# Attention's output products placed in the bank of the softmax sums, in halves between later score units; six buffers of probabilities in place of eight

## The chip, the cores and the metric

The kernel runs on one core of a Trainium2 chip (trn2). The metric is the device time of one execution in microseconds (us). One more execution was taken with the hardware profiler; all lines of profiles below come from such an execution. PE is TensorE (matmuls), DVE is VectorE, ACT is ScalarE, POOL is GpSimd, SP is the engine whose queue issues most DMAs.

## The reference, cut to what matters

The program is two transformer layers over 2048 tokens of width 512 in float32. Layer 0 is linear attention beside a mixture of experts, layer 1 is causal attention within a window beside a second block that works on selected tokens. The change lies in the last part of layer 1, its attention with 16 heads of 32:

```python
mask = (q_idx >= k_idx) & (q_idx - k_idx <= WINDOW)          # WINDOW = 1024
scores = jnp.einsum('bhqd,bhkd->bhqk', q, k) / np.sqrt(HD)
scores = jnp.where(mask[None, None, :, :], scores, NEG)
attn = jax.nn.softmax(scores, axis=-1)
out = jnp.einsum('bhqk,bhkd->bhqd', attn, v)
out = out.transpose(0, 2, 1, 3).reshape(b, n, H)
return jnp.einsum('bnh,hm->bnm', out, w_out)
```

The result of that last product is added to everything else that layer 1 computes (kept in a DRAM tensor `res_d`) and written out.

## The kernel before, in words

Queries, keys and the row maxima of the scores are ready (transposed, on chip) when the last stage begins. It works on **groups** `(Q, g)`: Q is a block of four query tiles (512 queries), g a set of four heads. The order of groups is (2,0), (0,0), (2,1), (0,1), (2,2), (0,2), (2,3), (0,3), then (1,0) to (1,3), then (3,0) to (3,3). A group is a list of **units**, each one block of 128 keys against up to 512 queries: nine units for Q=2 and Q=3, four for Q=0, eight for Q=1.

For each unit the loop does this:

- `probabilities` (L1300 scores on PE, L1315 the negated maxima added by a matmul, L1323 the masks added by a matmul) fills two score tiles `ps`, each two PSUM banks; `ps_s` has three such buffers. ACT takes the exponential into SBUF (L1334): into `acc` for the first unit of a group, into `pt` for the others. `pt` has eight buffers, two a unit.
- `values` (L1374) multiplies the previous unit's probabilities with V into `av`, one PSUM bank that a group keeps. After the last unit ACT copies it into `aT` (L117).
- `gathered` (L1407) adds the previous unit's probabilities into `acc`, on POOL for odd units and on DVE for even ones, both halves one after the other. For Q=2 and Q=3 the last unit goes straight into the sums on PE.
- `ending` of the previous group is a generator, advanced once a unit: three empty steps, then the sums over keys by a matmul with ones (L1388) into `sm`, a single PSUM bank, then for each query tile a reciprocal (L1417) and a multiplication of `aT` (L1418), two tiles a step. If the group was the last of its query block (g=3), the four `output`s follow, one a step.
- `output` (L1337 to L1349) loads a tile of `res_d` (two buffers `res`), multiplies `aT` with `w_out` in four matmuls (L1344) into `po`, which is one of the three score buffers, adds `res` on DVE (L1348) and stores.

The units are software pipelined: in the turn of unit n PE runs the scores of n, then the values of n-1, then what `ending` holds. When the last unit of a group is through, whatever is left of the group before's ending is run to its end. Groups of Q=0 have four units, so the ending of (2,3) is still at its reciprocals when (0,3) is over, and all four outputs of Q=2 are then issued together. The outputs of Q=0 come in the units of (1,0), those of Q=1 in the units of (3,0), those of Q=3 after the last unit.

[...] A layer that records the program settles the order of each engine's instructions when the kernel is built; it may place an instruction some places away from where the source has it. A buffer of a pool is handed on when the last instruction that used it has ended, by a semaphore wait of the new user.

Of the kernel before, what the change touches and what calls it, by code (L numbers as in the profile page):

```python
# [12 lines left out]
F32 = mybir.dt.float32  # L13
# [6 lines left out]
P = 128  # L20
T = 2048
NT = T // P
D = 512
NC = D // P
# [14 lines left out]
def two_layer_kernel(ctx: ExitStack, tc: tile.TileContext, a: dict, out: bass.AP):  # L39
# [29 lines left out]
    def load(eng, dst, src):  # L69
        eng.dma_start(out=dst, in_=src)  # L70
# [57 lines left out]
    with ExitStack() as l0:  # L128
# [208 lines left out]
        with ExitStack() as p3:  # L337
            wk = p3.enter_context(tc.tile_pool(name="wk3", bufs=2, reuse_waits="tile"))
# [5 lines left out]
            def mm(name):  # L344
                return ps.tile([P, TB], F32, tag="mm", name=name)
# [119 lines left out]
            for b in range(NTB):  # L465
# [39 lines left out]
                if b == NTB - 1:  # L505
# [3 lines left out]
                    def pool(name, bufs):  # L509
                        return p4.enter_context(  # L510
                            tc.tile_pool(name=name, bufs=bufs, side="right", reuse_waits="tile")
                        )
# [33 lines left out]
                for i in range(TB // P):  # L546
# [4 lines left out]
                    po = mm(f"po_{b}_{i}")  # L551
# [171 lines left out]
    with p4:  # L723
        wka, r5, wk = pool("wka", 2), pool("r5", 1), pool("wk4", 2)
# [272 lines left out]
    with ExitStack() as p5:  # L997
        f5 = p5.enter_context(tc.tile_pool(name="f5", bufs=1, side="right", reuse_waits="tile"))
        fw = p5.enter_context(tc.tile_pool(name="fw", bufs=5, side="right", reuse_waits="tile"))
        wk = p5.enter_context(tc.tile_pool(name="wk6", bufs=2, side="right", reuse_waits="tile"))  # L1000
# [223 lines left out]
        for ch in range(NFC):  # L1224
            wd = stream(a["w_down"][ch * D : (ch + 1) * D, :], f"wd_{ch}")
            for i in range(NC):
                f = ch * NC + i
# [34 lines left out]
        )  # L1262
    w_out = const([P, NC, D], "w_out", vo_pool)
    load(nc.sync, w_out, a["w_out"].rearrange("(c p) o -> p c o", p=P))
    pt = ctx.enter_context(tc.tile_pool(name="pt", bufs=8, reuse_waits="tile"))
    acc_pool = ctx.enter_context(tc.tile_pool(name="acc_pool", bufs=2, reuse_waits="tile"))
    wk = ctx.enter_context(tc.tile_pool(name="wk7", bufs=2, reuse_waits="tile"))
    ps_s = ctx.enter_context(tc.tile_pool(name="ps_s", bufs=3, **tight))
    ps_v = ctx.enter_context(tc.tile_pool(name="ps_v7", bufs=1, **tight))

    QT = 4
# [63 lines left out]
            got.append(pT)  # L1335
        return got

    def output(i, aT, j0):
        rows = slice(i * P, (i + 1) * P)
        res = wk.tile([P, D], F32, tag="res", name=f"res_{i}")  # L1340
        load(nc.sync, res, res_d[rows, :])
        po = ps_s.tile([P, D], F32, tag="s", name=f"po_{i}")
        for g in range(NC):
            PE.matmul(  # L1344
                po, aT[:, g, j0 : j0 + P], w_out[:, g, :], start=g == 0, stop=g == NC - 1
            )
        o = wk.tile([P, D], F32, tag="o", name=f"o_{i}")
        V.tensor_tensor(o, po, res, ALU.add)  # L1348
        load(nc.sync, out[rows, :], o)  # L1349

    class Group:

# [55 lines left out]

        def ending(self):

            Q, g, aT = self.Q, self.g, self.aT
            for _ in range(3):
                yield
            self.sums(self.acc, 0, QT * P, True)
            for j in range(QT):
                js = slice(j * P, (j + 1) * P)
                V.reciprocal(self.sm[:, js], self.sm[:, js])  # L1417
                V.tensor_tensor(aT[:, g, js], aT[:, g, js], self.sm[:, js], ALU.mult)  # L1418
                if j % 2:
                    yield  # L1420
            if g == NC - 1:
                for j in range(QT):
                    output(QT * Q + j, aT, j * P)
                    yield

    pending, ending = None, iter(())

# [2 lines left out]
    outputs = {}  # L1430
    for Q, g in order:
        if g == 0:
            outputs[Q] = wk.tile([P, NC, QT * P], F32, tag="aT", name=f"aT_{Q}")
        group = Group(Q, g, outputs[Q])
        for n, unit in enumerate(group.us):
            name = f"{Q}_{g}_{n}"
            got = probabilities(g, unit, name, n == 0)
            if (Q, g, n) == (2, 0, 1):

                early.place(ps_s, "s", 0.0)  # L1440
                early.turned()
            if pending is not None:
                pending[0].values(*pending[1:])
                pending[0].gathered(*pending[1:])
                if pending[1] == len(pending[0].us) - 1:
                    for _ in ending:
                        pass
                    ending = pending[0].ending()
            next(ending, None)
            pending = (group, n, got)  # L1450
# [3 lines left out]
        pass  # L1454
    for _ in group.ending():
        pass


def _rope(n, dim):
# [48 lines left out]
```

## Time and profile before

| what | value |
|---|---|
| median of 3 runs | 1708.75 us (1707.05 to 1709.91) |
| the profiled execution | 1708.32 us, span 1706.6 us |
| mean granted clock of TensorE | 0.995 |
| instructions | 20413 |
| last stage, from the first score matmul at 1328.0 us | about 378 us |
| its scores, L1300 | 1152 records, 139.9 us busy |
| its values from `pt`, L1374 | 1024 records, 100.8 us busy |
| its exponentials, L1334 | 208 into `pt`, 181.6 us busy |
| its accumulations, L1407 | POOL 110, 252.8 us; DVE 80, 144.4 us |

How to read a profile: the page gives busy times of each engine, then the chain of work that ended last, then the costliest groups of instructions, each by line of the kernel, engine, operation, tiles and shape. A timeline line gives the start and the duration in us, then engine, line, operation, tiles, shapes and how many instructions were merged (float32 matmuls are recorded as two), and in brackets the time that the engine was idle before it and what ended that. A row by stage gives the length of a stretch, the busy time of PE, of PE's weight loads, of DVE, ACT and POOL (with counts), then the granted clock of TensorE as a share of full speed, then DMA.

### The profile page before, as it was taken

Reading aid. Unit: us, or ns where it says so; the run is one execution under the profiler, and the core shown is the slowest. Engines: PE = TensorE matmul, PEld = TensorE weight load, DVE = VectorE, ACT = ScalarE, POOL = GpSimd, SP = SyncE. Lnnn points to the kernel's source line nnn. Section 1 sums busy time; section 2 is a strip of 40 time slices with the busy share of each in tenths; the row PEclk is TensorE's granted clock in tenths of the full one; section 3 lists DMA queues with packets and bytes.
Section 4 is the critical chain, followed back from the end, with each engine's and each line's share of the span. In section 5 each row is a group of like instructions: output and inputs, shape, how many; then the busy total and the mean of one; then the engine's idle time right before and its main releaser. Section 6 shows DMA issues by size and latency. Waiting matters only on the chain.

```text
span 1706.6 us, 20413 instructions
## 1 busy us (share of the span) xinstructions
PE 1656.3 (97%) x8114; PEld 742.5 (44%) x8114; DVE 982.1 (58%) x1256; ACT 589.3 (35%) x939; POOL 499.5 (29%) x398
## 2 busy tenths in 40 slices
PE   8999999999999999989999989999999999999999
PEld 3445444444444444444443434454564333433343
DVE  4754746344444544356676676775554477556565
ACT  3213333243253344212121110440100576447473
POOL 3230000000000200043565425230000677558584
PEclk9999999999999999999999999999899999999999
DMA  9411001120030421121010024112222300110101
GB/s 361 170 38 47 25 25 37 45 92 25 25 111 25 94 104 50 50 69 50 32 26 32 28 99 173 62 50 74 75 99 75 99 1 2 50 51 2 50 1 38
DMA packets 62384, 109.23 MB, mean 64 GB/s; under 512 B 12528, under 2 KB 14064, under 8 KB 61520
## 3 DMA queue, kind: packets, MB, share of 16 engines
q1 hardware_dynamic: 55856, 106.12, 18.2%
q0 software_dynamic: 1152, 1.21, 0.4%
q10 hardware_dynamic: 5280, 0.59, 0.4%
q8 instruction: 63, 1.03, 0.2%
q14 instruction: 33, 0.27, 0.1%
HBM read 86.24 MB, written 21.67 MB: 63 GB/s over the span
## 4 chain that ended last, share of the span: by engine, by line
PE 80%; DVE 11%; ACT 2%; DMA 2%; POOL 2%; issue 2%; SPq 0%; DVEq 0%; POOLq 0%; ACTq 0%
PE acc L478 6%; PE eg L492 6%; PE ea L494 6%; PE ps L1300 6%; PE pa L633 6%; PE av L1374 6%; PE p L965 5%; PE po L553 3%; PE pq L367 3%; PE po L1344 3%; PE gx L242 3%; DVE mx L645 3%; PE mg L1214 2%; PE pao L1176 2%; PE pm L1229 2%
## 5 line engine op out<-in xcount | busy, mean ns | idle before, releaser
L645 DVE TENSOR_REDUCE mx<-pa 128x4 f32<-128x1536 f32 (+3 forms) x144 | 252.8, 1756 | 151.7 <-PE pa L641 71.9
L1407 POOL TENSOR_TENSOR acc<-acc,pt 128x1024 f32<-128x1024 f32 (+2 forms) x110 | 252.8, 2327 | 96.6 <-DVE acc L1407 43.3
L1334 ACT ACTIVATE pt<-ps 128x1024 f32<-128x1024 f32 (+3 forms) x208 | 181.6, 925 | 107.9 <-PE ps L1323 61.4
L1407 DVE TENSOR_TENSOR acc<-acc,pt 128x1024 f32<-128x1024 f32 (+1 forms) x80 | 144.4, 1833 | 103.9 <-POOL acc L1407 103.9
L633 PE MATMUL pa<-kT,qT 32*128 32x384 f32 (+3 forms) x1152 | 139.4, 539 | 19.5 <-DVE mx L645 15.8
L350 ACT ACTIVATE r_e<-eg 128x512 f32<-128x512 f32 x128 | 76.0, 595 | 201.6 <-PE eg L492 194.8
L1300 PE MATMUL ps<-qT,kT 32*128 32x512 f32 (+3 forms) x1152 | 139.9, 524 | 0.0
L352 DVE TENSOR_TENSOR h<-ea,r_e 128x512 f32<-128x512 f32 x128 | 87.3, 684 | 85.2 <-ACT r_e L351 84.6
L743 POOL TENSOR_TENSOR cosg<-cosg,gam 128x512 f32<-128x512 f32 x2 | 2.5, 1269 | 442.7 <-DVE gam L740 442.7
L492 PE MATMUL eg<-xl,rwgT 128*128 128x512 f32 x256 | 130.7, 592 | 0.0
L494 PE MATMUL ea<-xw,rw1T 128*128 128x512 f32 x256 | 130.7, 592 | 0.0
L478 PE MATMUL acc<-h,rw2T 128*128 128x512 f32 x256 | 129.3, 592 | 0.0
L965 PE MATMUL p<-w_qk,xnt 128*128 128x512 f32 x256 | 123.7, 606 | 2.3 <-DVE qk L758 2.2
L1374 PE MATMUL av<-pt,v 128*32 128x512 f32 (+3 forms) x1024 | 100.8, 482 | 0.0
L1300 PEld LDWEIGHTS ps<-qT,kT 32*128 32x128 f32 x1152 | 54.7, 183 | 94.7 <-issue 65.8
L633 PEld LDWEIGHTS pa<-kT,qT 32*128 32x128 f32 x1152 | 46.7, 184 | 103.7 <-DVE mx L645 66.8
L488 DVE TENSOR_TENSOR xw<-xw,xl 128x512 f32<-128x512 f32 x64 | 43.8, 685 | 82.8 <-DMA xw<-w_d 82.7
L351 ACT ACTIVATE r_e<-r_e 128x512 f32<-128x512 f32 x128 | 80.5, 631 | 5.7 <-ACT r_e L350 1.9
L494 PEld LDWEIGHTS ea<-xw,rw1T 128*128 128x128 f32 x256 | 48.6, 190 | 61.2 <-issue 59.3
L492 PEld LDWEIGHTS eg<-xl,rwgT 128*128 128x128 f32 x256 | 48.6, 190 | 61.2 <-issue 60.7
L478 PEld LDWEIGHTS acc<-h,rw2T 128*128 128x128 f32 x256 | 48.6, 190 | 61.2 <-issue 54.7
L763 POOL TENSOR_TENSOR t<-qk,cosg 128x1024 f32<-128x1024 f32 x15 | 35.3, 2353 | 99.6 <-DVE qk L758 63.4
(336 smaller groups left out, 2444.2 us busy)
## 6 DMA issues: line engine op xcount, KB each, us to landing
xw<-w_d SPq DMA_DIRECT2D x64, 256.0 KB, 3.2
x<-in_x SPq DMA_DIRECT2D x16, 256.0 KB, 4.3
res_d<-x SPq DMA_DIRECT2D x16, 256.0 KB, 2.6
xr<-res_d SPq DMA_DIRECT2D x16, 256.0 KB, 4.1
xn_d<-xn SPq DMA_DIRECT2D x16, 256.0 KB, 3.0
res_d<-xr SPq DMA_DIRECT2D x16, 256.0 KB, 3.1
xnq<-xn_d SPq DMA_DIRECT2D x16, 256.0 KB, 2.7
v_d<-vt SPq DMA_DIRECT2D x16, 256.0 KB, 2.0
```

What stands on the lines that cost most here:

```text
L351: S.activation(r, r, AF.Square)
L352: V.tensor_tensor(dst, pa, r, ALU.mult)
L478: PE.matmul(acc, rw2T[:, j, e, :], h, start=e == 0 and j == 0, stop=e == E - 1 and j == 1,)
L492: PE.matmul(pg, rwgT[:, e, hb], xl, start=True, stop=True)
L494: PE.matmul(pa, rw1T[:, e, hb], xw, start=True, stop=True)
L633: PE.matmul(pS[:, h, : w * P], qT[r, g, i * P : (i + 1) * P], kT[r, g, ks], start=True, stop=not (edge or last),)
L645: V.tensor_reduce(mx[:, g, :, c], pS[:, :, : w * P], AX.X, ALU.max)
L965: PE.matmul(pj, xnt[:, c, :], w, start=c == 0, stop=c == NC - 1)
L1300: PE.matmul(pS[h // 2][:, h % 2, t0 * P - q0 : (t1 + 1) * P - q0], kT[r, g, kb * P : (kb + 1) * P], qT[r, g, t0 * P : (t1 + 1) * P], start ...
L1334: S.activation(pT[:, :, :n], pS[hp][:, :, :n], AF.Exp)
L1374: PE.matmul(self.av[h * HD : (h + 1) * HD, t0 * P - o : (t1 + 1) * P - o], vs[kb // 4][:, kb % 4, hs], got[h // 2][:, h % 2, t0 * P - q0 : ...
L1407: eng.tensor_tensor(part, part, got[hp][:, :, : q1 - q0], ALU.add)
```

## The change

- `output` becomes a generator of two halves: a load of `res`, the allocation of `po` and two of the four matmuls, then (one step later) the other two, the addition and the store. Its PSUM tile is given by the caller.
- When a group of g=3 ends, its four outputs are put on a list `ready`. Each later `ending` takes up to two of them after its own reciprocals, into the bank of the sums (`ps_v`, tag `sm`). So the outputs of Q=2 and Q=0 run in the endings that pass through (1,0), (1,1), (1,2) and (1,3) (on into the group that follows), those of Q=1 in (3,1) and (3,2). What is left at the end, the four of Q=3, runs in score buffers as before.
- When a group is through, the rest of the ending before it is run ahead of `gathered`, not behind it, since for Q=2 and Q=3 `gathered` of a last unit takes the bank of the sums.
- `pt` has six buffers in place of eight; `aT` has three in place of two, since an attention output now lives on into later groups. The two sizes cancel in SBUF.

```diff
-    pt = ctx.enter_context(tc.tile_pool(name="pt", bufs=8, reuse_waits="tile"))
+    pt = ctx.enter_context(tc.tile_pool(name="pt", bufs=6, reuse_waits="tile"))
...
-    def output(i, aT, j0):
+    def output(i, aT, j0, pool, tag):
+
         rows = slice(i * P, (i + 1) * P)
         res = wk.tile([P, D], F32, tag="res", name=f"res_{i}")
         load(nc.sync, res, res_d[rows, :])
-        po = ps_s.tile([P, D], F32, tag="s", name=f"po_{i}")
+        po = pool.tile([P, D], F32, tag=tag, name=f"po_{i}")
         for g in range(NC):
             PE.matmul(
                 po, aT[:, g, j0 : j0 + P], w_out[:, g, :], start=g == 0, stop=g == NC - 1
             )
+            if g == 1:
+                yield
         o = wk.tile([P, D], F32, tag="o", name=f"o_{i}")
         V.tensor_tensor(o, po, res, ALU.add)
         load(nc.sync, out[rows, :], o)
+        yield
+
+    ready = []
...
+            for _ in range(min(2, len(ready))):
+                yield from output(*ready.pop(0), ps_v, "sm")
             if g == NC - 1:
-                for j in range(QT):
-                    output(QT * Q + j, aT, j * P)
-                    yield
+                ready.extend((QT * Q + j, aT, j * P) for j in range(QT))
...
-            outputs[Q] = wk.tile([P, NC, QT * P], F32, tag="aT", name=f"aT_{Q}")
+            outputs[Q] = wk.tile([P, NC, QT * P], F32, tag="aT", name=f"aT_{Q}", bufs=3)
...
                 pending[0].values(*pending[1:])
-                pending[0].gathered(*pending[1:])
-                if pending[1] == len(pending[0].us) - 1:
+                last = pending[1] == len(pending[0].us) - 1
+                if last:
                     for _ in ending:
                         pass
+                pending[0].gathered(*pending[1:])
+                if last:
                     ending = pending[0].ending()
...
+    for args in ready:
+        for _ in output(*args, ps_s, "s"):
+            pass
```

## The prediction

> **What bounds the kernel now.** I read the page first (busy shares, then the chain that ended last), then the busy time by stage, the waits of PE, and last the order of time around one output projection.
>
> ```profile
> PE 1656.3 (97%) x8114; PEld 742.5 (44%) x8114; DVE 982.1 (58%) x1256; ACT 589.3 (35%) x939; POOL 499.5 (29%) x398
> ...
> PE 80%; DVE 11%; ACT 2%; DMA 2%; POOL 2%; issue 2%; SPq 0%; DVEq 0%; POOLq 0%; ACTq 0%
> ```
>
> PE is the engine to watch. The change touches only the last stage, from about 1328 us. Its row by stage, and the waits of PE in it:
>
> ```profile
> core 0: us, PE busy (x) PEld busy (x) DVE busy (x) ACT busy (x) POOL busy (x), PEclk, DMA share, GB/s
> 1328.00:1706.00 378.00, 372.69 (x3405) 142.45 (x3404) 232.30 (x227) 220.29 (x257) 255.44 (x112) 1.00 0.10 33
> ```
>
> ```profile
> engine line waited for: us in total, times, longest us
> PE po L1344 <- DVE o L1348: 1.5, 2, 1.3
> ```
>
> PE is busy for 372.69 of 378 us. Of the 5.3 us idle, about 4 are the drain after the last matmul and 1.5 are two waits of an output projection for the addition of an earlier one. So the end is the sum of what PE executes, in its own order; a microsecond that PE stands still is a microsecond on the time, and the most that a better order can return is small.
>
> Now one group with outputs, Q=1, g=0 (units n=0 to 7). First PE, then DVE, same microseconds:
>
> ```profile
> 1483.79 1.06 PE L1374 MATMUL av<-acc,v 128*32 128x512 f32 x8
> 1484.79 1.36 PE L1300 MATMUL ps<-qT,kT 32*128 32x512 f32 x8
> ...
> 1489.51 1.04 PE L1388 MATMUL sm<-acc,ones_f 128*32 128x512 f32 x8
> ...
> 1494.35 1.06 PE L1374 MATMUL av<-pt,v 128*32 128x512 f32 x8
> 1495.34 3.70 PE L1344 MATMUL po<-w_out,aT 128*128 128x512 f32 x8
> 1498.97 0.71 PE L1300 MATMUL ps<-qT,kT 32*128 32x256 f32 x8
> ```
>
> ```profile
> 1487.45 4.51 DVE L1407 TENSOR_TENSOR acc<-acc,pt 128x1024 f32<-128x1024 f32 x2 [4.14 <-POOL acc L1407]
> 1491.88 0.95 DVE L1417 RECIPROCAL sm<-sm 128x128 f32<-128x128 f32 x1
> ...
> 1495.83 0.97 DVE L1417 RECIPROCAL sm<-sm 128x128 f32<-128x128 f32 x1
> 1496.71 1.21 DVE L1407 TENSOR_TENSOR acc<-acc,pt 128x1024 f32<-128x1024 f32 x1
> 1497.83 0.27 DVE L1418 TENSOR_TENSOR aT<-aT,sm 128x128 f32<-128x128 f32 x1
> ```
>
> PE has written the sums by 1490.5, but DVE is still inside unit 2's accumulation until 1491.95, then walks through four reciprocals and multiplications, with a piece of unit 4's accumulation ahead of the fourth multiplication. It leaves the bank of the sums at 1498.10. PE came to the output at 1495.34 and started, because its target is one of the three score buffers.
>
> **The change, part by part.**
>
> *Work.* The same 16 outputs: 64 matmuls, 3.63 us of PE each output (1495.34 to 1498.97), 16 additions of 0.69 us, 16 loads and 16 stores. Nothing is added or removed; the last four outputs stay at the end with their tail. In SP's queue the loads still stand two ahead, and the next load behind a store is needed a group later, so no load becomes late.
>
> *Where they go.* Two outputs in each of the groups (1,0), (1,1), (1,2), (1,3), (3,1), (3,2), in halves of 1.82 us ahead of units 6, 7, 8 and of the unit after (for Q=1, which has eight units, the last two are the next group's units 0 and 1). I checked this on the built order of instructions.
>
> *The added wait.* The first half now needs the bank of the sums, so it waits for DVE's fourth multiplication (in the built program that is the instruction it waits for). From the end of the values product of unit 0 I count both paths. PE to the output's place: 1484.79 to 1495.34 = 10.55 us (10.51 in (1,1), 10.77 in (3,1), read in the same way). DVE: unit 1's accumulation on POOL starts at 1485.05, unit 2's on DVE ends 6.90 us later at 1491.95, the fourth multiplication 6.15 us after that: 1498.10, so 13.3 us (13.3 in (1,1) and in (3,1)). With about 0.1 us from DVE to PE (sums at the end start 0.12 us after the accumulation they wait for), PE stands still 13.4 - 10.55 = 2.85 us in each of four Q=1 groups and 13.4 - 10.77 = 2.65 us in two Q=3 groups: 11.4 + 5.3 = **16.7 us**. Behind the waiting matmul on PE are unit 6's scores, for which ACT, POOL and DVE wait in turn; nothing else feeds PE. The bounds: zero if DVE were done in time; 4 to 5 us each if accumulation lags as it does in (1,2) and (1,3) of before, where the fourth multiplication came 14.4 and 15.6 us after unit 0's values. I take 2.85, because the stall and the 7.3 us of outputs let POOL and DVE catch up before the next group.
>
> *The second wait.* The second output waits for the first one's addition, which in DVE's order stands behind both accumulations of unit 6. For Q=1 these end 5.75 us after the fourth multiplication (1550.66 to 1556.41 in (1,2)); with the addition 6.4 us. PE, after the stall, comes back after 1.82 + 1.87 + 1.82 + 1.39 = 6.9 us (the two stretches between are 1565.57 to 1567.44 and on to 1568.83). For Q=3 the same rows of (3,2) and (3,1) give 8.6 against 1.82 + 2.96 + 1.82 + 2.84 = 9.4 us. Covered in both, by 0.5 to 0.8 us: I take 0, bound 0.5 each (3 us in all). The sums of a Q=3 group's last unit wait for the second addition, done 0.8 us after its product, while PE has 2.5 us of other work ahead: 0.
>
> *What goes away.* The two waits in (3,0), 1.47 us. Also a hidden one: at a boundary between groups, unit 1's stretch on PE takes 3.11 us (1551.96 to 1555.07) against 2.28 where an output stood before it (1515.10 to 1517.38), because PE waits inside its matmuls for ACT's exponentials and copy. A half output now covers it at three boundaries, (1,1) to (3,0): -2.5 us. At (0,3) to (1,0), where the burst of four outputs (14.0 us at 1468.58) covered it, it appears: +0.83. Together **-3.1 us**. The burst itself had PE busy throughout, so dissolving it returns nothing.
>
> *Six buffers.* An exponential now waits for the accumulations of three units before, not four. Laying the exponentials' starts beside the accumulations' ends, in the Q=2 groups only the first has late ones: unit 8's second half starts at 1353.14, its buffer would be free at 1354.39; two more are late by 0.2 and 0.4 us. In the late Q=1 groups up to 2 us are late in before, but there the outputs now push the exponentials back by over 4 us. I take **+0.5 us**, bounds 0 and 2.
>
> *The clock.* A still PE can lose its clock. Windows of 3.4 us of before, and what followed:
>
> ```profile
> 765.36:768.76 3.40, 1.49 (x17) 1.02 (x18) 2.32 (x5) 0.19 (x1) 3.32 (x3) 1.00 0.00 0
> 768.77:772.17 3.40, 3.40 (x17) 1.58 (x16) 0.80 (x1) 1.57 (x3) 0.45 (x1) 0.50 0.04 11
> ...
> 908.72:912.12 3.40, 1.60 (x7) 0.50 (x9) 3.26 (x4) 0.47 (x1) 0.00 (x0) 1.00 0.01 2
> 912.13:915.53 3.40, 3.40 (x18) 1.59 (x11) 2.71 (x3) 0.59 (x1) 3.22 (x2) 1.00 0.02 5
> ```
>
> A gap of 2.69 us (before 767.27) left PE 1.49 us of work in a window of 3.4, and for the next 3.4 us the granted clock was 0.50. Of six such windows with 1.47 to 1.61 us of work, three were followed by 0.50 (the other two begin at 1000.88 and 1195.44). The Trainium skill ("TensorE: Matmul & The Clock Gate", Part 1: The HAM clock gate) halves the clock only after an idle window of about 3.4 us; by it a stall of 2.8 us is safe and this item is 0. The trace shows gaps of 1.8 to 2.7 us punished, so I follow the trace. A stall of 2.8 us placed at random against windows of 3.4 us leaves less than about 1.6 us of work in one of them in two cases of three: an estimate of 4 halved stretches from 6 stalls, each costing half of the 3.0 us or so that lie after the stall, 1.5 us: **+6.0 us**; bounds 0 and 6 x 1.7 = 10.
>
> *Sum.* 16.7 - 3.1 + 0.5 + 6.0 = 20.1 us. The profiled execution took 1708.32 us (span 1706.6), 0.4 us under the median of 1708.75, so against the median: 1708.75 + 20.1 = 1728.9, **1729 us**.
>
> **The rivals.**
>
> - *Stalls at full clock.* The skill's rule holds here, at most one stretch is halved: 20.1 - 6.0 = 14.1, so 1722.9 us. For it: three windows of 1.5 to 1.6 us of work went unpunished.
> - *No stall, not slower.* DVE leaves the bank in time, and only the removed waits count: -3.1 + 0.5 = -2.6, 1706.1 us. This needs DVE's 13.3 us after unit 0's values to shrink under 10.5, by more than two of the 1.3 us reciprocal steps; from there each group is free. For it: the accumulations of 2.3 us hold 1.2 us of work when POOL is quiet (1496.71). Against: POOL's accumulation of unit 3 runs beside them as before, and four groups of before show the 6.15 us after unit 2 unchanged.
> - *Six buffers bind.* If each of four Q=2 groups loses the first one's worst 1.25 us, that is +5 in place of 0.5, with the stalls as above: 1733.4 us. Against: the later three groups show 0.3 us or more of slack.
>
> **How the numbers follow.** A run of three can tell about 0.2%, 3.4 us, from no change. Chances: forecast 0.66, stalls at full clock 0.17, six buffers binding too 0.08, no stall 0.09. The last ends at -0.15%, within 0.2% or just beyond with less cost of buffers: same 0.05, faster 0.04. Slower is 0.91. The range: below, the full-clock case with stalls of 2 us instead of 2.8 gives 1718; above, six halved stretches and 0.5 us at every second wait give 1729 + 4 + 3 = 1736. I state 1718 to 1736, which leaves out the case without stalls and some tails.
>
> **What would show it.** In the profile of the changed kernel: waits of the output matmul for DVE's sums multiplication, six of 2.6 to 2.9 us, 16 to 17 in all; the waits for the output's addition near 0; granted clock 0.50 for 3.4 us after some of these; the stretch of unit 1 at 2.28 us in (1,2), (1,3) and (3,0); ACT waiting for POOL under 2 us. The forecast is wrong if those waits are absent or under 1 us (DVE's chain shortens), if the clock stays at 1.00 after all six, or if PE waits for ACT in the Q=2 groups.

## The result, and the profile after

The changed kernel takes 1733.63 us (median of 4 runs, 1730.32 to 1738.48). The kernel before, run beside it, takes 1709.33 us (4 runs, 1707.05 to 1710.17). The ratio is 1.0148, with a 95% interval of 1.0134 to 1.0162: some 24 us slower. The forecast was 1729 us. The profiled executions are those of 1708.32 us (span 1706.6) and 1730.32 us (span 1728.6).

First the page of the changed kernel: busy shares of the engines, then the chain that ended last.

```profile
PE 1661.9 (96%) x8114; PEld 741.2 (43%) x8114; DVE 972.9 (56%) x1256; ACT 588.4 (34%) x939; POOL 497.8 (29%) x398
...
PE 79%; DVE 11%; DMA 2%; issue 2%; POOL 2%; ACT 2%; SPq 0%; DVEq 0%; ACTq 0%; POOLq 0%
```

PE executes the same 8114 instructions and is still the engine that sets the end, but it is now busy for 5.6 us more, and it stands still. The last stage alone, by busy time, and the waits of PE in it:

```profile
core 0: us, PE busy (x) PEld busy (x) DVE busy (x) ACT busy (x) POOL busy (x), PEclk, DMA share, GB/s
1325.52:1728.60 403.08, 382.53 (x3405) 142.83 (x3404) 222.94 (x227) 220.23 (x257) 253.61 (x112) 0.98 0.10 31
```

```profile
engine line waited for: us in total, times, longest us
PE po L1345 <- DVE aT L1425: 16.3, 6, 2.8
```

From its first score matmul to the end of the span the stage takes 403.1 us in place of 378.6, so **24.5 us** more. Six waits make 16.3 us of that; the two waits of before, for an addition, are gone. PE's busy time in the stage grew by 9.8 us, although its work is the same and its granted clock is down from 1.00 to 0.98.

One group with outputs, (1,1), in order of time. First PE, then DVE in the same microseconds.

```profile
1506.43 1.07 PE L1380 MATMUL av<-pt,v 128*32 128x512 f32 x8
...
1509.00 1.07 PE L1380 MATMUL av<-pt,v 128*32 128x512 f32 x8
1512.86 3.06 PE L1345 MATMUL po<-w_out,aT 128*128 128x512 f32 x4 [2.80 <-DVE aT L1425]
1515.85 1.23 PE L1300 MATMUL ps<-qT,kT 32*128 32x256 f32 x8
...
1518.28 1.98 PE L1345 MATMUL po<-w_out,aT 128*128 128x512 f32 x4
1520.19 0.50 PE L1300 MATMUL ps<-qT,kT 32*128 32x128 f32 x8
```

```profile
1502.16 4.50 DVE L1413 TENSOR_TENSOR acc<-acc,pt 128x1024 f32<-128x1024 f32 x2 [4.15 <-POOL acc L1413]
1506.59 0.95 DVE L1424 RECIPROCAL sm<-sm 128x128 f32<-128x128 f32 x1
...
1511.41 1.21 DVE L1413 TENSOR_TENSOR acc<-acc,pt 128x1024 f32<-128x1024 f32 x1
1512.54 0.27 DVE L1425 TENSOR_TENSOR aT<-aT,sm 128x128 f32<-128x128 f32 x1
...
1518.25 1.29 DVE L1413 TENSOR_TENSOR acc<-acc,pt 128x512 f32<-128x512 f32 x2 [4.31 <-ACT pt L1334]
1520.30 0.69 DVE L1351 TENSOR_TENSOR o<-po,res 128x512 f32<-128x512 f32 x1 [0.75 <-PE po L1345]
```

The fourth multiplication of the sums ends at 1512.81 and the output starts at 1512.86. PE was there 2.80 us earlier. Once the stall is paid, everything after it is in time: DVE is done with unit 6's accumulation before the first output's second half ends, and the addition at 1520.30 follows that half at once. Note also the two half outputs: the first lasts from 1512.86 to 1515.85, 2.99 us, the second from 1518.28 to 1520.19, 1.91 us. Most of the first ran at half clock. Rows by stretch of the trace of after: a stall and what follows it, another stall and what follows it, and what follows a third:

```profile
1479.50:1482.90 3.40, 0.59 (x5) 0.22 (x2) 3.33 (x6) 0.81 (x2) 1.84 (x2) 1.00 0.00 0
1482.92:1486.30 3.38, 3.38 (x8) 0.85 (x7) 0.84 (x1) 0.00 (x0) 3.38 (x2) 0.50 0.02 5
...
1571.66:1575.07 3.41, 1.98 (x8) 0.75 (x8) 2.51 (x4) 0.00 (x0) 2.09 (x1) 1.00 0.00 0
1575.07:1578.48 3.41, 3.41 (x28) 1.41 (x28) 1.64 (x2) 1.09 (x2) 2.54 (x2) 1.00 0.00 0
...
1626.28:1633.00 6.72, 5.91 (x24) 2.29 (x24) 1.89 (x3) 0.00 (x0) 5.69 (x2) 0.50 0.00 0
```

Four of the six stalls are followed by a granted clock of 0.50: for 3.41 us from 1482.91, 1513.63 and 1544.35, and for 6.83 us from 1626.27. After the stalls at 1570.57 and 1662.76 (2.52 us each) the clock stays at 1.00. PE is busy for about 16.2 of these 17.1 us, and half of that, 8.1 us, is lost. The last section comes back to why four and not six.

### The profile page after: what moved, and what is told of

Read it like the earlier page. It is cut to its first block, busy times and chain, and to the rows that moved or that the text cites. A ratio compares the mean times of both kernels' runs of the same rounds, so it can differ in the third digit from the quotient of the medians.

```text
span 1728.6 us, 20425 instructions
## 1 busy us (share of the span) xinstructions
PE 1661.9 (96%) x8114; PEld 741.2 (43%) x8114; DVE 972.9 (56%) x1256; ACT 588.4 (34%) x939; POOL 497.8 (29%) x398
## 4 chain that ended last, share of the span: by engine, by line
PE 79%; DVE 11%; DMA 2%; issue 2%; POOL 2%; ACT 2%; SPq 0%; DVEq 0%; ACTq 0%; POOLq 0%
PE eg L492 6%; PE ea L494 6%; PE acc L478 6%; PE ps L1300 6%; PE pa L633 6%; PE av L1380 5%; PE p L965 5%; PE po L1345 4%; PE po L553 3%; PE pq L367 3%; PE gx L242 3%; DVE mx L645 3%; PE mg L1214 2%; PE pm L1229 2%; PE po L555 2%
## 5 line engine op out<-in xcount | busy, mean ns | idle before, releaser
L1413 DVE TENSOR_TENSOR acc<-acc,pt 128x1024 f32<-128x1024 f32 (+1 forms) x80 | 134.8, 1713 | 119.3 <-POOL acc L1413 85.9
L1345 PE MATMUL po<-w_out,aT 128*128 128x512 f32 x128 | 66.6, 655 | 16.3 <-DVE aT L1425 16.3
```

Source lines behind the costliest of these rows:

```text
L1345: PE.matmul(po, aT[:, g, j0 : j0 + P], w_out[:, g, :], start=g == 0, stop=g == NC - 1)
L1413: eng.tensor_tensor(part, part, got[hp][:, :, : q1 - q0], ALU.add)
```

## The experiments

Eleven kernels were run. They ask in turn: are the stalls and the clock what the time is made of; what makes the bank late; is it the bank alone; and is there something in the change that is worth keeping. Each ratio is against the kernel before, run beside it. "The stage" is always the time from the first score matmul of the last stage to the end of the span, in the profiled execution: 378.6 us before, 403.1 us after.

### Six buffers alone (e2_before6)

The kernel before, with one size changed:

```diff
-    pt = ctx.enter_context(tc.tile_pool(name="pt", bufs=8, reuse_waits="tile"))
+    pt = ctx.enter_context(tc.tile_pool(name="pt", bufs=6, reuse_waits="tile"))
```

> The kernel before with six probability buffers and nothing else. My theory (the slow-down is the wait of the outputs for the bank of the sums, and the clock that is lost after it): between 0 and +2 us against before (late exponentials in the first Q=2 group and in the Q=1 groups, part of it hidden), ACT's wait for POOL in the last stage rises from 1.1 to 3 to 8 us, PE's only wait stays that for the addition (1.5 us). Rival (six buffers are what costs): +10 us or more.

Measured: 1710.71 us, ratio 1.0007 (0.9999 to 1.0014). ACT waits for POOL's accumulations 2.7 us in all and PE shows no wait. The stage takes 379.7 us, 1.1 us more, of which the groups (1,2) and (1,3) take 1.0 and 1.2 us more and (3,0) 1.7 us less. The four groups of Q=2 together take 0.3 us more. Six buffers are not where 24 us went.

### The stalls filled with work (e3_fill)

The changed kernel, with three matmuls of no use into a score buffer ahead of the first output of each of the six groups, so that PE is kept busy while the bank of the sums is held:

```diff
+            if ready:
+                fill = ps_s.tile([P, 2, QT * P], F32, tag="s", name=f"fill_{Q}_{g}")
+                for c in range(3):
+                    PE.matmul(
+                        fill[:, 0, :], w_out[:, c, 0:P], w_out[:, c, :], start=c == 0, stop=c == 2
+                    )
             for _ in range(min(2, len(ready))):
                 yield from output(*ready.pop(0), ps_v, "sm")
```

> The changed kernel with three extra matmuls (2.7 us, into a score buffer that nobody reads) just ahead of the first output of each of the six groups, so that PE works while it would stand still. The result is not changed. Theory that part of the loss is the granted clock: the six waits shrink to about 0.1 us each, no stretch of 0.50 follows them, mean clock back to 0.995, and the time falls by 6 to 9 us from the changed kernel's 1733.6 to about 1726, and its runs lie closer together. Rival (the clock costs nothing, all is the wait itself): the time stays within 2 us of 1733. Second rival (PE's order is not the bound): the added 16 us of matmuls make it slower.

Measured: 1727.31 us, ratio 1.0106 (1.0092 to 1.0121). PE in the group (1,1) of this kernel:

```profile
1510.53 2.84 PE L1431 MATMUL fill<-w_out 128*128 128x512 f32 x6
1513.38 1.98 PE L1345 MATMUL po<-w_out,aT 128*128 128x512 f32 x4
1515.30 0.71 PE L1300 MATMUL ps<-qT,kT 32*128 32x256 f32 x8
```

The fill takes the place of the stall (2.84 us against 2.80), and the output starts the moment it ends. No stretch of the stage is at half clock. The stage takes 395.2 us: 7.9 us less than in the changed kernel, though the order of the real work and the time until the bank comes free are the same. That is about what the half clock costs. The stage is still 16.6 us longer than before: the six fills, which only keep PE busy until the bank is free, make 17.0 us, and the small terms summed up under "Why the prediction was right" (-3.1, +0.2, +2.3) make the rest, to within 0.2 us.

### The outputs one unit later (e4_late1)

```diff
+            if ready:
+                yield
             for _ in range(min(2, len(ready))):
                 yield from output(*ready.pop(0), ps_v, "sm")
```

> The changed kernel with one more empty step ahead of the outputs of a group, so that PE comes to the bank of the sums one unit later. Theory: the wait in the Q=1 groups falls from 2.8 to 0.9 us each (unit 6's stretch of 1.87 us lies before it), in the Q=3 groups to 0, and the sums of a Q=3 group's last unit now wait some 0.9 us for the second addition, twice; all waits of PE 5 to 6 us, no halved clock, time about 1712. Rival (spreading the outputs is itself what costs, or the six buffers): stays above 1725.

Measured: 1716.09 us, ratio 1.0033 (1.0020 to 1.0045); no half clock in the stage. Waits of PE in it:

```profile
PE po L1345 <- DVE aT L1425: 3.4, 4, 0.9
```

A unit of scores and values (1.87 us for Q=1, more for Q=3) goes into the stall: 2.5 to 2.8 us become 0.6 to 0.9 in the four groups of Q=1, and the two of Q=3 have none. The stage takes 384.2 us, 5.6 us more than before. The waits explain 3.4 of it; in (3,1) and in (3,2) two score matmuls ahead of the last unit's sums last 1.05 us where they take some 0.3 (the sums follow the second output's addition by 0.25 us), which the list of waits does not show: about 1.5 us for both. In the groups of Q=1 the second output now stays whole (3.70 us at 1495.00, for one), since the group is over before its halves get separate turns. So eight outputs are in halves and cost 1.5 us (the price of halves is given under "Why the prediction was right"). With +0.2 and -3.1 from there too, that makes 3.5 us; 2.1 us I could not assign.

### The bank alone, at the old places (e5_bank)

The kernel before, with all its outputs in the bank of the sums, whole and where they were (the last four, at the end of the kernel, too). As in the changed kernel, the rest of an ending is run ahead of `gathered`:

```diff
-        po = ps_s.tile([P, D], F32, tag="s", name=f"po_{i}")
+        po = ps_v.tile([P, D], F32, tag="sm", name=f"po_{i}")
...
-                pending[0].gathered(*pending[1:])
-                if pending[1] == len(pending[0].us) - 1:
+                last = pending[1] == len(pending[0].us) - 1
+                if last:
                     for _ in ending:
                         pass
+                pending[0].gathered(*pending[1:])
+                if last:
```

> The kernel before, with the outputs where they were and whole, eight buffers, but their products in the bank of the sums. Theory (the bank is the cause): slower than before by 16 to 25 us, about 1730: in the burst a wait of about 4 us for the multiplications and 0.9 us for each addition, in (1,0) about 3 us, in (3,0) about 5 us and 2 more, and one halved stretch of the clock after each longer wait. Rival (the spread over later groups is the cause): within 3 us of before.

Measured: 1739.61 us, ratio 1.0174 (1.0159 to 1.0188), so 30 us more, where 16 to 25 were expected. Waits of PE:

```profile
PE po L1344 <- DVE aT L1418: 14.3, 3, 6.0
PE po L1344 <- issue: 3.2, 1, 3.2
PE po L1344 <- DVE o L1348: 2.4, 3, 0.8
```

Without any spreading the bank costs 19.9 us of standing still. (The wait put down to "issue" ends at 1477.32, and the fourth multiplication of the sums ended at 1477.22, so it is one of the same kind.) The stage takes 409.9 us, 31.3 more than before; its granted clock is 0.50 in four stretches of 20.5 us in all. PE is busy for 16.5 us of them, so about 8 us of the 11.4 that the waits leave are lost there. 7.9 us of the waits are at the very end (5.5 us for the last multiplications and three additions of 0.8 us), which the changed kernel avoids by keeping the last four outputs in score buffers. This kernel's 1.0174 is therefore not to be read as the price of the bank in the changed one.

### One accumulation less on DVE (e8_no2)

The changed kernel without the accumulation of unit 2's probabilities, so a part of the softmax sums is not computed:

```diff
+            elif n == 2:
+                pass
```

> The changed kernel, but unit 2's probabilities are left out of the accumulation in every group (so a part of the softmax sums is not computed). DVE then comes to the reciprocals as soon as the sums are written, not behind unit 2's accumulation. Theory (the bank of the sums is held by DVE's queue; unit 2's accumulation there ends about 1 us after the sums are written): the waits of the output matmul for DVE's sums multiplication fall from 2.5-2.85 us to about 1.85 us (Q=1) and 1.6 us (Q=3), some 10.5 us in all in place of 16.3; fewer stretches at half clock; 1717 to 1721 us. Rival (POOL's accumulation of unit 3 beside the reciprocals sets their pace, or the clock is lost just the same): waits of 2.5 us or more, 1726 us or more.

Measured: 1717.04 us, ratio 1.0051 (1.0034 to 1.0069). The six waits for the multiplication are 1.58, 1.58, 1.58, 1.30, 1.31 and 1.31 us, 8.7 in all, and no stretch of the stage is at half clock. So DVE's queue does hold the bank: with the accumulation ahead of the reciprocals gone, they start when the sums are written. But a half of the stall is left, since four reciprocals and multiplications of 1.3 us each, with a piece of the next accumulation among them, are still longer than the two units that PE has in between.

### The sums two units earlier (e7_sums_early)

```diff
-            for _ in range(3):
+            early_sums = 2 if ready else 0
+            for _ in range(3 - early_sums):
                 yield
...
+            for _ in range(early_sums):
+                yield
             for _ in range(min(2, len(ready))):
                 yield from output(*ready.pop(0), ps_v, "sm")
```

> The changed kernel, but in the groups that have outputs the sums, reciprocals and multiplications come two units earlier; the outputs stay where they are. Theory (PE stands still only because the fourth multiplication ends about 2.8 us after PE's arrival): the fourth multiplication now ends about 2 us before PE arrives, so no wait for it and no stretch at half clock in this stage; the accumulations are pushed back behind the reciprocals, so the second output's wait for the first one's addition may show, 0 to 1.5 us in each of six groups. Time 1709 to 1717 us: before's 1709.4, - 3.1 for the boundaries, + 2.3 for outputs split in halves, + 0.5 for buffers, + 0 to 9 for the additions. Rival (the bank of the sums is late wherever the sums are made, because later units' accumulations then stand ahead of the reciprocals): waits of over 2 us remain, 1722 us or more.

Measured: 1734.99 us, ratio 1.0154 (1.0133 to 1.0174): the rival's number. Waits of PE in the stage:

```profile
PE po L1345 <- DVE o L1351: 15.5, 6, 2.8
PE sm L1394 <- DVE aT L1426: 1.3, 1, 1.3
```

The first output waits no more, as the theory had it. (The 1.3 us are the early sums of one group, which wait for the bank themselves.) But the second output now waits 2.2 to 2.8 us in each group, for the first one's addition, where I had expected 0 to 1.5, and four of these waits are followed by half clock. The addition stands in DVE's order behind unit 6's accumulation. The time is that of the changed kernel, with the stall at another place. So the stall at the sums was covering a second one; the next kernel has that second one alone.

### The same order in a score buffer (e9_scorebuf)

```diff
-                yield from output(*ready.pop(0), ps_v, "sm")
+                yield from output(*ready.pop(0), ps_s, "s")
```

> The changed kernel with one word changed: the spread half outputs are written into a score buffer, as before, and not into the bank of the sums. Halves, places, six buffers and the order of the instructions on every engine are those of the changed kernel. Theory (the bank is the cause): no wait of an output for DVE's sums multiplication and no stretch at half clock in the last stage; before's 1709.4 - 3.1 (boundaries and the two old waits) + 2.3 (halves) + 0.5 (six buffers) = 1709.1 us, plus what scores or second outputs wait because an output now holds one of the three score buffers for a unit: 0 to 1 us for each of 12 outputs, so 1709 to 1717 us, most of it in the groups of Q=3. Rival (spreading and splitting the outputs costs the time, whatever bank they use): 1722 us or more, with waits of over 2 us in each of the six groups.

Measured: 1724.35 us, ratio 1.0107 (1.0091 to 1.0123). The order of the instructions is the same as in the changed kernel on every engine; in the two traces DVE's 1256 stand in one and the same order. No output waits for the sums, yet PE waits 11.2 us in six places. The second output of (1,1), on PE, and what it waits for, on DVE:

```profile
1515.30 1.98 PE L1345 MATMUL po<-w_out,aT 128*128 128x512 f32 x4
...
1520.70 1.98 PE L1345 MATMUL po<-w_out,aT 128*128 128x512 f32 x4 [2.04 <-DVE o L1351]
```

```profile
1517.16 2.89 DVE L1413 TENSOR_TENSOR acc<-acc,pt 128x512 f32<-128x512 f32 x2 [1.70 <-POOL acc L1413]
1519.97 0.68 DVE L1351 TENSOR_TENSOR o<-po,res 128x512 f32<-128x512 f32 x1
```

The first output is complete at 1517.2. Its addition has to wait for unit 6's accumulation, which itself waited for POOL's of unit 5, and runs at 1519.97. The three score buffers go round: two tiles of unit 7's scores take the other two, and the second output gets the one that the first still holds. The time is the rival's (1722 us or more), but not for the rival's reason as written: with the bank out of play 1.0148 falls to 1.0107, and what is left is a wait for something else. My theory lacked that wait: it had 0 to 1 us for an output, where the first one's buffer is held 2 us too long.

### The second output one step later, in a score buffer (e10_gap)

```diff
+            for k in range(min(2, len(ready))):
+                if k:
+                    yield
                 yield from output(*ready.pop(0), ps_s, "s")
```

> The kernel e9_scorebuf with an empty step between the first and the second output of each group: the first output is still two halves ahead of units 6 and 7, the second comes whole, behind the last values of the group. Theory (all that is left of the loss in e9_scorebuf is that PE reaches the second output 2 us before DVE, behind unit 6's accumulation, has added the first; the scores and the values that PE now does in between take 2.4 us for Q=1 and more for Q=3): no wait of an output above 0.3 us, no stretch at half clock in the last stage, PE's own work as in the kernel before but for the split of six outputs (+1.2), the boundaries and the two old waits (-3.1) and six buffers (+0.5): 1709.4 - 1.4 = 1708 us, between 1706 and 1710. Rival (DVE's additions drift back with PE, so the wait only moves on): waits of 1 us or more in most of the six groups, 1714 us or more.

Measured: 1733.05 us, ratio 1.0130 (1.0105 to 1.0155), runs from 1723.07 to 1734.88. The theory failed. PE in (1,1):

```profile
1521.65 1.67 PE L1300 MATMUL ps<-qT,kT 32*128 32x512 f32 x8 [2.03 <-DVE o L1351]
```

I had moved the second output out of the way and forgotten that the buffer goes to whoever comes next: now it is the scores of the next group's unit 0 that wait, for the same addition and for the same time (11.2 us in six places in both kernels). In the groups of Q=1 the second output comes whole (5.75 us at half clock, at 1524.80), in those of Q=3 still in halves. Its stage takes 402.7 us all the same, 10.9 more than that of e9_scorebuf, because of the clock, to which the last section returns.

### Whole outputs, in the two banks (e11_whole_s, e12_whole_bank)

What the halves do to the order on DVE is now the suspect: the addition of a whole output comes ahead of unit 6's accumulation, that of a halved one behind it. Both kernels are the changed one without the step inside an output; e12 keeps the bank of the sums (the first edit alone), e11 takes score buffers (both):

```diff
-            if g == 1:
-                yield
...
-                yield from output(*ready.pop(0), ps_v, "sm")
+                yield from output(*ready.pop(0), ps_s, "s")
```

> The changed kernel with two things undone: outputs are whole again (four matmuls in one step) and are written into score buffers. Places by groups (two outputs in each of six groups, from unit 6 on), six buffers of probabilities and three of aT stay. On DVE the addition of the first output now stands ahead of unit 6's accumulation, as in the kernel before, and not behind it. Theory (the losses come from the bank of the sums and from the halving, which puts the addition behind unit 6's accumulation; spreading the outputs over the groups costs nothing): no wait above 0.5 us; the two old waits go (-1.5), boundary (0,3) to (1,0) loses its cover (+0.8), the others don't gain, six buffers +0.5: 1709.4 - 0.2 = 1709 us, 1708 to 1711. Rival (outputs two at a time between units delay scores or waits wherever they are written): waits of 1 us or more in most of the six groups, 1716 us or more.

> The changed kernel with the halving alone undone: whole outputs (four matmuls in one step), in the bank of the sums. Theory (the bank alone makes the first output wait for DVE's fourth sums multiplication, whatever its length): six waits of 2.5 to 2.9 us as in the changed kernel, about 16.3 us; no wait of the second output above 0.5 us; -1.5 for the two old waits, +0.8 for boundary (0,3) to (1,0), +0.5 for buffers, and 0 to 10 us for stretches at half clock: 1726 to 1736 us. Rival (it is the halving that makes the bank late): waits under 1.5 us each, 1718 us or less.

Measured: e11_whole_s 1709.88 us, ratio 1.0004 (0.9995 to 1.0013), no wait of PE in the stage; e12_whole_bank 1736.83 us, ratio 1.0159 (1.0140 to 1.0178), with half clock after each of its six waits:

```profile
PE po L1345 <- DVE aT L1423: 16.3, 6, 2.9
```

DVE in (1,1) of e11_whole_s:

```profile
1512.16 0.27 DVE L1423 TENSOR_TENSOR aT<-aT,sm 128x128 f32<-128x128 f32 x1
1512.35 1.22 DVE L1411 TENSOR_TENSOR acc<-acc,pt 128x1024 f32<-128x1024 f32 x1
1513.49 0.68 DVE L1349 TENSOR_TENSOR o<-po,res 128x512 f32<-128x512 f32 x1
1515.28 2.88 DVE L1411 TENSOR_TENSOR acc<-acc,pt 128x512 f32<-128x512 f32 x2 [1.11 <-POOL acc L1411]
```

The addition at 1513.49 comes before unit 6's accumulation at 1515.28, and the score buffer is free when the next tile needs it. PE had started this output at 1509.62, 2.81 us before the fourth multiplication ended. Only the bank of the sums would have made it wait: its own `aT` is that of an earlier query block. The four kernels with the same two outputs in each of six groups, side by side:

| | in the bank of the sums | in a score buffer |
|---|---|---|
| in halves | the changed kernel: 1.0148; waits 16.3 us, for the sums; stage 403.1 | e9_scorebuf: 1.0107; waits 11.2 us, for the addition; stage 391.8 |
| whole | e12_whole_bank: 1.0159; waits 16.3 us, for the sums; stage 405.9 | e11_whole_s: 1.0004; none; stage 379.2 |

Spreading the outputs costs nothing that the runs can tell, and neither do the six buffers, the third `aT` or the moved rest of the endings, all of which e11_whole_s has. Either the bank or the halves alone is enough for a stall in each group, and with both only the first one, at the sums, shows.

### Only the places that gain (e6_edge)

The kernel before, with its whole outputs, score buffers and eight buffers of probabilities, and its burst of four for Q=2. The other outputs are issued at boundaries between groups: those of Q=0 one each into (1,1), (1,2), (1,3) and (3,0), those of Q=1 two each into (3,1) and (3,2):

```diff
-            if g == NC - 1:
+            if g == NC - 1 and Q < 2:
+                ready.extend((QT * Q + j, aT, j * P) for j in range(QT))
+            elif g == NC - 1:
                 for j in range(QT):
                     output(QT * Q + j, aT, j * P)
                     yield
...
                     ending = pending[0].ending()
+                    for _ in range(min(len(ready), 2 if (Q, g) > (3, 0) else 1)):
+                        output(*ready.pop(0))
```

> The kernel before, with whole outputs in score buffers and eight buffers of probabilities; only the places differ: Q=2's four stay in their burst; Q=0's four are issued one each at the boundaries into (1,1), (1,2), (1,3) and (3,0), right behind the last values of the group before; Q=1's four two each at the boundaries into (3,1) and (3,2). Theory (an output at a boundary hides PE's wait for ACT's exponentials, 0.83 us each, and needs nothing from the bank of the sums): unit 1's stretch at 2.28 us in place of 3.11 at three boundaries, -2.5 us, and the 1.47 us of waits in (3,0) go: -4.0 us, 1705.4 us. Rival (the wait inside the boundary comes back one unit later, or the output's three buffers delay the next scores): within 0.1% of before, 1709 us.

Measured: 1704.06 us (9 runs) against 1709.04 us (14 runs), ratio 0.9970 (0.9959 to 0.9980). It is 0.3% faster than the kernel before, and faster than the changed one. The stage takes 374.2 us, 4.4 us less than before, and PE has no wait in it. PE at the boundary into (1,2):

```profile
1541.46 3.70 PE L1344 MATMUL po<-w_out,aT 128*128 128x512 f32 x8
1545.09 1.14 PE L1300 MATMUL ps<-qT,kT 32*128 32x512 f32 x8
...
1546.38 1.06 PE L1374 MATMUL av<-acc,v 128*32 128x512 f32 x8
1547.37 1.30 PE L1300 MATMUL ps<-qT,kT 32*128 32x512 f32 x8
```

Unit 1's stretch, 1545.09 to 1547.37, takes 2.28 us; without the output ahead of it, in the kernel before, it was 3.11.

## Why the prediction was right

The direction, the mechanism and the place were as forecast, and the time lies inside the range, 4.6 us above the point. Its steps, one by one:

- **PE sets the end.** Right. In e3_fill and in the four kernels of the table, what PE waits (or fills), the half clock and the small terms below add up to the stage's growth to 1.3 us or less.
- **The added wait, 16.7 us.** Measured 16.3: 2.81, 2.80, 2.79 and 2.52 us in the groups of Q=1, 2.85 and 2.52 in those of Q=3. The forecast's own sign was 2.6 to 2.9, so two fell a little short. In (1,1) the two lengths counted in the profile of before held: from unit 0's values 13.4 us by way of DVE (1499.49 to 1512.86) and 10.6 on PE (1499.49 to 1510.07). e8_no2 shows that DVE's queue is what holds the bank: with unit 2's accumulation out, the wait falls to 1.3 to 1.6 us. e11_whole_s against e12_whole_bank shows that it is the bank.
- **The second wait, 0.** Right for this kernel, and only because the first stall is there. In (1,3), at full clock, the first output's addition ends 6.55 us after the fourth multiplication (forecast: 6.4), and PE comes back after 7.1 (6.9). The step gave it 0.5 to 0.8 us of cover *after* the stall; take away 2.8 us of stall, and about 2 us should be missing. e9_scorebuf has 2.04 us, e7_sums_early 2.2 to 2.8. I did not draw that conclusion at the time.
- **What goes away, -3.1 us.** Right: in the changed kernel unit 1's stretch takes 2.29 us at the boundaries into (1,2), (1,3) and (3,0) (1527.38 to 1529.67, for one) and 3.11 us at that into (1,0) (1466.25 to 1469.36). e6_edge, which has the gain and not the loss, comes to -4.4 us where the same terms give -4.0.
- **Six buffers, +0.5 us.** Alone +1.1 us in the profiled stage, and no difference that the runs could tell (1.0007). In the changed kernel the eight groups of Q=2 and Q=0 together take 0.2 us more, and ACT's waits for POOL stay at 1.1 us.
- **The clock, +6.0 us.** The number of halved stretches was right, four, and that is partly luck: e12_whole_bank has six waits of the same lengths, and all six were followed by half clock. Also, by the forecast's own figures a stall of 2.8 us leaves under 1.6 us of work in a window in three cases of four, not two of three, which is 4.6 stretches. Their cost was under-sized: about 8 us (7.9 by e3_fill; half of 16.2 us by the rows), since one stretch lasted 6.83 us, and the others were filled to the end. Following the trace of before, and not the rule of the Trainium skill ("TensorE: Matmul & The Clock Gate", Part 1: The HAM clock gate), by which it would have been 0, was right: here the clock was halved after stalls of 2.79 to 2.85 us.
- **"Nothing is added or removed."** Here the sum lacks a term. A half output takes 1.91 us (1518.28 to 1520.19), where half of a whole one was taken, 1.82. Two of them take 3.82 us against 3.63, so twelve outputs cost 2.3 us more, 0.19 each.

With the measured sizes the sum is 16.3 - 3.1 + 0.2 + 8.1 + 2.3 = 23.8 us, against 24.5 us in the stage and 24.3 between the medians. The forecast's 20.1 us was short by the clock (2) and by the halves (2.3); 0.7 us of the stage stay unassigned.

**The rivals.** *Stalls at full clock* (1722.9 us) fell: the stalls cost a clock. *Six buffers bind* fell with e2_before6; the time near its 1733.4 us has other causes. *No stall, not slower* (1706.1 us) was wrong in its premise and in its price. e7_sums_early is that case, with the bank free in time, and it takes 1734.99 us. I had written that from there each group is free; the next wait in line on DVE had not been counted for the case in which the first one is gone.

## What to carry to other kernels

Before you give a tile to another pool, ask of each buffer who held it last and what stands ahead of that holder on its engine; a single bank shared with a slow chain makes its next user as late as the chain, however small the user is. When a stall is removed, or is put at zero in a rival, redo the count for every later hand-over without it, since a stall gives the engines behind it time to catch up. Splitting a matmul group moves its consumer in another engine's order too: here two halves put a 0.7 us addition behind an accumulation, and that cost as much as the bank.

## What the runs showed of the hardware

The half clock does not depend on the gap's length alone. Rows of e9_scorebuf, then of e10_gap, around stalls of the same length (2.04 and 2.03 us):

```profile
1519.01:1522.42 3.41, 1.72 (x4) 0.68 (x4) 1.64 (x3) 0.00 (x0) 1.73 (x2) 1.00 0.23 81
1522.42:1525.83 3.41, 3.41 (x28) 1.48 (x28) 0.00 (x0) 1.60 (x2) 0.00 (x0) 1.00 0.26 77
```

```profile
1518.72:1522.13 3.41, 1.38 (x17) 0.63 (x20) 2.88 (x3) 0.66 (x2) 2.72 (x3) 1.00 0.00 0
1522.14:1525.54 3.40, 3.40 (x25) 1.23 (x18) 0.00 (x0) 1.43 (x2) 0.12 (x1) 0.50 0.51 158
1525.55:1528.95 3.40, 3.40 (x5) 1.35 (x4) 0.00 (x0) 0.98 (x2) 0.00 (x0) 0.50 0.00 1
```

The first goes on at full clock, the second at half clock for 6.83 us. In e10_gap this happens after each of the four stalls of Q=1; in e9_scorebuf after one of six, for 3.41 us. PE is busy throughout, and half of each stretch is lost: about 13.7 us against 1.7. The difference of 12.0, less 0.8 for the four outputs that e10_gap leaves whole, is 11.2 us, against 10.9 between the two stages; the waits are 11.2 us in both.

The clock changes on a fixed grid. Within each of the thirteen traces all its changes lie whole multiples of 3.413 us apart, to within 0.01 us. In the changed kernel, for one, three halved stretches of the last stage begin at 1482.91, 1513.63 and 1544.35, each time nine steps (30.72 us) apart. The rows above are cut on the grid of their own trace, and so are the counts that follow. Of the grid's windows in the last stage, all traces together, 23 at full clock were followed by half clock; PE was busy in them for 0 to 1.66 us. The other 1402 were followed by full clock; PE was busy for 1.68 us or more in all of them but one, which had 1.50. So what goes with the half clock is how little PE did in one window of the grid, and a stall can fall into one window or lie across two. The stall of e10_gap above (1519.62 to 1521.65) lies within one and leaves 1.38 us of work; that of e9_scorebuf (1518.67 to 1520.70) begins in the window before and leaves 1.72. In the changed kernel the four stalls that were followed by half clock leave 0.6 to 1.4 us, the two others 1.95 and 1.98. A stall of 1.6 us leaves at least 1.8 us in any window in which PE is busy otherwise, and after stalls of that length or less (e8_no2, e4_late1) the clock was never halved in this stage.

A group that lasts nearly nine steps of the grid brings its stall to nearly the same place each time: of the four stalls in the groups of Q=1, e12_whole_bank (a group each 30.6 us) and e10_gap (30.8) lose their clock after four, the changed kernel (30.1) after three, e9_scorebuf (27.8 to 29.4) after one.

The limits: no run moved a stall against the grid and changed nothing else, so this is a reading of thirteen traces and not an experiment. And it holds for this stage: earlier in the program windows with 1.4 to 1.9 us of work went either way, and a few with 2.4 to 2.5 us were followed by half clock (that of e12_whole_bank from 141.98, for one), so busy time is not the whole measure. Why e10_gap's half clock lasts two windows, though PE is busy for all of the first, no run shows either. Where the grid lies would account for the spread between runs of one kernel: the changed one took 1730.32 us at a mean clock of 0.993 and 1738.48 at 0.988, e10_gap 1723.07 at 0.994 and 1734.88 at 0.987.

The second surprise is the 0.1 us for each piece into which a float32 output group of four matmuls is cut (3.63 us whole, 2 x 1.91 in halves). e3_fill and e9_scorebuf show the same 1.91 to 1.92 us. Whether it is lost at the start or at the end of a piece, the trace doesn't tell.
